# Range checks split and moved, and sums products over two key blocks, in the banded-attention layer of a two-layer kernel

## Chip, cores and metric

The kernel runs on one core of one Trainium2 chip. The time is device microseconds of one execution, and the figure that counts is the median over runs. A core has TensorE (PE in the profile; its weight loads are PEld), VectorE (DVE), ScalarE (ACT), GpSimd (POOL), and SyncE (SP), which issues the DMAs here.

## What is computed

Two layers act on an image of 128 x 256 positions with 256 channels. Each adds an attention over group-normalised input to its input. The first has eight heads, a bias from a second input, a mask and a gate. The change is in the second:

```python
def _L1_conv_ref(x, w_in, b_in, w_out, b_out, band):     # band = 16, H = 4 heads of D = 64
    x2 = x.reshape(B * T, F, C)                          # 128 rows of F = 256 positions, C = 256
    qkv = x2 @ w_in.T + b_in
    q, k, v = jnp.split(qkv, 3, axis=-1)                 # then split into heads
    scores = jnp.einsum('bhid,bhjd->bhij', q, k) / jnp.sqrt(D)
    keep = jnp.abs(i - j) <= band
    scores = jnp.where(keep, scores, -jnp.inf)
    attn = jax.nn.softmax(scores, axis=-1)
    out = jnp.einsum('bhij,bhjd->bhid', attn, v)
    y = out @ w_out.T + b_out

x = x + _L1_conv_ref(_gn(x), ..., 16)
```

Everything is float32.

## The kernel before

The kernel is a fast path with a verdict: it takes exponentials without subtracting a maximum, and checks on the way that the quantities which could leave the safe range did not. Each check leaves a one or a zero per partition in a column of a tile `ok`. At the very end the smallest of them, reduced over the partitions by a product with `ones`, becomes the integer `verdict`; all engines load it and branch to a general kernel if a check failed.

Layer 1 works on pairs of rows, 64 pairs, in a loop over `p` whose order of instructions is written out by hand (`manual_schedule`): each engine runs its instructions in the order of the Python text. In one pass the loop holds three pairs at once. `was` is the pair before, whose second row is still to be applied and put out; `now` is the pair whose scores are taken; `nxt` is the pair whose queries, keys and values are made; `nn` and `n3` are loaded, turned and centred ahead.

The steps that the change touches, or that its effect runs through:

- `scores(r)`: for each row, 256 keys in four blocks of 64. A block's keys meet only `W` = 96 queries, from `q0(k)` on. ScalarE takes the exponential, GpSimd multiplies by the band's ones and zeros (`e<-e,bw`, L1980).
- `apply(r)` (L1998): on tiles of 64 x 32 of the PE array, the products of the values and the exponentials. Even and odd blocks go to different PSUM tiles (`o_eo[0]`, `o_eo[1]`), since neighbours overlap. A third turn of the outermost loop, `a == 2`, multiplies by ones instead of values and gives the softmax sums, into the first half of `su_y`. Every float32 product appears as two matmul records.
- `copy_sums`, `copy_odd` (ScalarE), `join_sums`, `join_odd` (VectorE, L2019 and L2022) add the odd blocks to the even ones; `invert` (L2025) is the reciprocal of the sums; `weigh` (L2030) multiplies the outputs by it.
- `out_block`, `out_row` (L2046) multiply by `w_out` into the second half of `su_y`; `keep_row` (L2054) adds the residual, and the output leaves by DMA.
- `product(n, i)` and `join(n, i)` (L1912 and L1916; L1932): seven products in place of eight for each of queries, keys and values (n = 0, 1, 2). Each n has two PSUM tiles, and a product that starts anew in one waits until its last reader is done.
- `centre`, `differences`, `add_bias`, `turn`: preparing later pairs, on ScalarE (L1865), GpSimd (L1878 to L1881 and L1871) and VectorE (the transpose, L1860).

A check is three VectorE instructions (L958 to L960): a comparison with the lower bound, a `scalar_tensor_tensor` that compares with the upper bound and multiplies, and a minimum. The quantities: the exponentials of the bias (`eb`, 16 checks of 256 columns), the mask (1), the reciprocals of layer 0's sums, loaded again from DRAM (8), and those of layer 1's pairs 0 to 55, also loaded again (4, the last of 128 columns). They wait in the list `checks`, and one is taken out in each pass with `p > 0`, between `nn.centre(0)` and `now.apply(0)`. The last `LATE` = 8 pairs are checked from the tile in place, by `guard`, just ahead of that: 512 columns at once in the loop, and twice 256 columns at the very end.

Of the kernel before, what the change touches and what calls it, by code (L numbers as in the profile page):

```python
# [16 lines left out]
P = 128  # L17
# [756 lines left out]
def fast_kernel(  # L774
# [173 lines left out]
    kb = const.tile([P, KC], F32, name="kb")  # L948
    vb_r = const.tile([P, C], F32, name="vb_r")
    bz_r = const.tile([P, H], F32, name="bz_r")  # L950
    ok = const.tile([P, 48], F32, name="ok")
    done = []

    def check(src, lo, hi, pool):

        n = src.shape[1]
        a = pool.tile([P, 512], F32, name="chk", tag="chk", bufs=1)[:, :n]
        nc.vector.tensor_scalar(a, src, lo, None, ALU.is_gt)  # L958
        nc.vector.scalar_tensor_tensor(a, src, hi, a, ALU.is_lt, ALU.mult)  # L959
        nc.vector.tensor_reduce(ok[:, len(done) : len(done) + 1], a, AX.X, ALU.min)  # L960
        done.append(src)

    def group_pairs(src, g):

# [796 lines left out]
    def q0(k):  # L1761
        return min(max(k * KB - BAND, 0), I - W)

    def half(k):
        return slice((k % 2) * KB, (k % 2 + 1) * KB)
# [15 lines left out]
    with tc.tile_pool(name="l1", bufs=2) as sb, tc.tile_pool(  # L1781
# [54 lines left out]
        class Pair1:  # L1836
# [148 lines left out]
            def apply(self, r):  # L1985


                e = self.es[r]
                for a in range(3):
                    for j in range(NK // 2):  # L1990
                        for h in range(H1):
                            for k in (2 * j, 2 * j + 1):
                                at = slice(h * DH, (h + 1) * DH)
                                n = k % 2
                                to = o_eo[n][at, a, q0(k) : q0(k) + W] if a < 2 else su_eo[n][at, q0(k) : q0(k) + W]
                                w = (self.v[half(k), r, j, h * D1 + a * DH : h * D1 + (a + 1) * DH] if a < 2
                                     else ones[half(k), :DH])
                                nc.tensor.matmul(  # L1998
                                    to, w, e[half(k), h % 2, h // 2, j * W : (j + 1) * W], start=True, stop=True,
                                )  # L2000

            def guard(self, r):
                if self.p == NP - 1:
                    check(self.rv[:, r, :], 1e-16, 1e8, sm)
                elif r == 1 and self.p >= NP - LATE:
                    check(self.rv.rearrange("p r i -> p (r i)"), 1e-16, 1e8, sm)

            def copy_sums(self, r):
                if r == 0:
# [17 lines left out]
            def weigh(self, r):  # L2027
                rv, odd = self.rv, self.odd
                oT = sb.tile([P, 2, I], F32, name="oT1", tag="oT", bufs=3)
                nc.vector.tensor_tensor(oT, odd, bcast(rv[:, r, :], 1, 2), ALU.mult)  # L2030
                self.oT[r] = oT
                if r == 1 and self.p < NP - LATE:
                    nc.sync.dma_start(rsum1[self.p].rearrange("q r i -> q (r i)"), rv[0:P:DH].rearrange("q r i -> q (r i)"))

# [31 lines left out]

        checks = []

        def check_all(src, lo, hi):
            for i in range(0, src.shape[1], 256):
                n = min(256, src.shape[1] - i)
                checks.append(lambda i=i, n=n: check(src[:, i : i + n], lo, hi, sm))

        def load_sums(src, name):
            t = sb.tile([P, src.shape[0] // P], F32, name=name, tag=name, bufs=1)
            nc.sync.dma_start(t, src.rearrange("(a b) -> a b", a=P))
            check_all(t, 1e-16, 1e8)

        with tc.manual_schedule():
            now, nxt = pair1(0), pair1(1)
            now.turn()
            norm1()
            mix_weights()
            for k in range(KC):
                now.centre(k)
            nxt.turn()
            for m in range(KC):
                now.project("qT", m)  # L2090
                now.project("kT", m)
                nxt.centre(m)
            nxt.differences()
            for r in range(2):
                now.values(r)
            now.add_bias()
            nxt.add_bias()
            check_all(eb.rearrange("p h b i -> p (h b i)"), math.exp(-20.0), math.exp(20.0))

            was = Nobody()  # L2100
            for p in range(NP - 1):
                nn = pair1(p + 2) if p == 0 else n3
                n3 = pair1(p + 3)
                if p == 0:
                    nn.turn()
                if p == 1:
                    mask_t = sb.tile([S, I], F32, name="mask_all", bufs=1)
                    nc.sync.dma_start(mask_t, mask)
                    check_all(mask_t, 1e-15, 1e15)
                    load_sums(rsum.rearrange("n q r c i -> (n q r c i)"), "sums0")  # L2110
                if p == NP - LATE + 2:
                    load_sums(rsum1[: NP - LATE].rearrange("n q r i -> (n q r i)"), "sums1")

                now.scores(0)
                now.scores(1)
                was.apply(1)
                nxt.begin_fast()
                was.copy_sums(1)
                nxt.product(0, 1)
                was.copy_odd(1)  # L2120
                nxt.product(1, 1)
                was.join_sums(1)
                for n in range(2):
                    nxt.product(n, 2)
                    nxt.join(n, 2)
                was.invert(1)
                for i in (6, 5, 7):
                    for n in range(2):
                        nxt.product(n, i)
                for n in range(2):  # L2130
                    nxt.join(n, 5)
                was.join_odd(1)
                was.weigh(1)
                was.out_row(0)
                for n in range(2):
                    nxt.product(n, 4)
                    nxt.product(n, 3)
                    nxt.join(n, 3)
                fast = p < NP - 2
                if fast:  # L2140
                    nxt.product(2, 1)
                    nxt.product(2, 2)
                    nxt.join(2, 2)
                nn.centre(0)
                was.guard(1)
                if checks and p > 0:
                    checks.pop(0)()

                now.apply(0)
                now.copy_sums(0)  # L2150
                if fast:
                    nxt.product(2, 6)
                    nxt.product(2, 5)
                now.copy_odd(0)
                now.join_sums(0)
                was.out_block(1, 0)
                if fast:
                    nxt.product(2, 7)
                now.join_odd(0)
                was.out_block(1, 1)  # L2160
                if fast:
                    nxt.join(2, 5)
                was.keep_row(1)
                if fast:
                    nxt.product(2, 4)
                    nxt.product(2, 3)
                    nxt.join(2, 3)
                now.invert(0)
                now.weigh(0)
                nn.centre(1)  # L2170
                nn.differences()
                nn.add_bias()
                n3.turn()
                was, now, nxt = now, nxt, nn
            assert not checks

            now.scores(0)
            was.apply(1)
            was.copy_sums(1)
            was.copy_odd(1)  # L2180
            now.values(0)
            was.join_sums(1)
            was.join_odd(1)
            was.invert(1)
            was.weigh(1)
            was.out_row(0)
            now.scores(1)
            now.values(1, 1)
            was.out_row(1)
            was.guard(1)  # L2190
            now.apply(0)
            now.copy_sums(0)
            now.copy_odd(0)
            now.join_sums(0)
            now.join_odd(0)
            now.invert(0)
            now.weigh(0)
            now.apply(1)
            now.copy_sums(1)
            now.copy_odd(1)  # L2200
            for b in range(NB):
                now.out_block(0, b)
            now.join_sums(1)
            now.invert(1)
            now.join_odd(1)
            now.weigh(1)
            now.keep_row(0)
            now.out_row(1)
            for r in range(2):
                now.guard(r)  # L2210

        tot = sm.tile([P, 1], F32, name="okmin", bufs=1)
        nc.vector.tensor_reduce(tot, ok[:, : len(done)], AX.X, ALU.min)
        ps = mm1("ok_ps")
        nc.tensor.matmul(ps[:, 0:1], ones, tot, start=True, stop=True)
        nc.vector.tensor_scalar(verdict, ps[0:1, 0:1], P - 0.5, None, ALU.is_lt)
# [65 lines left out]
```

## Time and profile before

| what | value |
|---|---|
| median of 3 runs | 3167.43 us (3166.82 to 3171.35) |
| the profiled execution | 3168.69 us, its span 3167.0 us |
| mean granted TensorE clock | 0.982 |
| layer 1's pair loop, from about | 2025 us to 3134 us |
| PE busy | 3027.1 us, 96% of the span |
| DVE busy | 2405.7 us, 76% |
| POOL busy | 2268.8 us, 72% |
| ACT busy | 1572.4 us, 50% |
| DVE instructions | 3983 |
| TensorE matmul records | 35678 |

The profile is of one execution. "Busy" counts the time in which an engine ran an instruction; matmuls are pipelined, so that a busy TensorE is not one at its peak. A line of a timeline gives the start and the length in us, the engine, the line of the kernel, the operation, what it writes and reads, the shapes, and in brackets how long the engine had been idle and what ended that. A line with `x4` merges four instructions. The chain of waits follows the end of the program back to what released each step.

### The profile page before, as it was taken

To read this page: it belongs to the slowest core of one execution; us is meant where nothing else is said; L and a number is where in the kernel's file an instruction comes from. 1 tells how busy PE (TensorE), PEld (TensorE's weight loads), DVE (VectorE), ACT (ScalarE), POOL (GpSimd) and SP (SyncE) were. 2 spreads that over 40 slices of the span, in tenths; PEclk is the share of its full clock that TensorE was granted. 3 is DMA by queue.
4 is the path that set the end of the run, shared out by engine and by line. 5 is a ranking of instruction groups with operands and counts; after the bars stand their busy time and mean duration, and the time that the engine had idled before them with its cause. 6 is when DMAs were issued, how large, how long until landed. Compare 5 with 4: busy or idle time off the path is not lost.

```text
span 3167.0 us, 84680 instructions
## 1 busy us (share of the span) xinstructions
PE 3027.1 (96%) x35678; PEld 2125.0 (67%) x35678; DVE 2405.7 (76%) x3983; ACT 1572.4 (50%) x2637; POOL 2268.8 (72%) x1632
## 2 busy tenths in 40 slices
PE   5579999999999999999999999899999999999997
PEld 3345555556555555556655555688888888888886
DVE  7976677777777777777777777588888777777776
ACT  3454444444444444444444443455555555555553
POOL 3459899889888899988988886455554555554543
PEclk9789999999999999999999999999999999999998
DMA  9952334333333334343243432544343434343431
GB/s 360 392 169 52 98 69 97 98 81 81 95 90 69 98 98 95 71 98 92 66 96 91 98 72 65 123 92 93 91 94 86 99 88 97 89 97 84 102 88 36
DMA packets 690967, 328.42 MB, mean 104 GB/s; under 512 B 538673, under 2 KB 639921, under 8 KB 689425
## 3 DMA queue, kind: packets, MB, share of 16 engines
q1 hardware_dynamic: 686176, 320.28, 40.2%
q8 instruction: 282, 4.62, 0.6%
q10 hardware_dynamic: 4400, 2.63, 0.3%
q14 instruction: 109, 0.88, 0.1%
HBM read 254.09 MB, written 68.75 MB: 102 GB/s over the span
## 4 chain that ended last, share of the span: by engine, by line
PE 87%; DVE 5%; DMA 2%; issue 2%; POOL 2%; ACT 1%; ACTq 0%; DVEq 0%; POOLq 0%; SPq 0%
PE ps_p L1357 21%; PE ps_qk L1916 12%; PE ps_sc L1394 8%; PE ps_ov L1429 7%; PE ps_su_y L2046 7%; PE ps_y L1484 7%; PE ps_v L1375 7%; PE ps_qk L1912 6%; PE ps_su L1437 3%; PE ps_sc L1969 3%; PE ps_o L1998 3%; DMA xa<-in_x_dram 1%; PE ps_su_y L1998 1%; DVE st L1192 1%; DVE chk L959 1%
## 5 line engine op out<-in xcount | busy, mean ns | idle before, releaser
L1418 POOL TENSOR_TENSOR eboth<-e 128x512 f32<-128x512 f32 x512 | 744.7, 1474 | 177.5 <-PE ps_su L1437 96.3
L1414 DVE TENSOR_TENSOR e<-ps_sc,eb 128x1024 f32<-128x1024 f32 x384 | 458.2, 1220 | 289.2 <-ACT ps_sc L1406 289.1
L1406 ACT ACTIVATE ps_sc<-ps_sc 128x1024 f32<-128x1024 f32 x384 | 375.4, 1007 | 436.5 <-PE ps_sc L1394 310.0
L1394 PE MATMUL ps_sc<-qT,kT 32*128 32x256 f32 x4096 | 294.1, 400 | 0.9 <-DVE e L1414 0.9
L1879 POOL TENSOR_TENSOR dT<-xgT,dT 128x256 f32<-128x256 f32 x63 | 45.9, 729 | 332.0 <-ACT xgT L1865 332.0
L2046 PE MATMUL ps_su_y<-w_out,oT 128*128 128x256 f32 x1008 | 257.7, 389 | 13.0 <-DVE sums L2019 11.8
L1980 POOL TENSOR_TENSOR e<-e,bw 128x384 f32<-128x384 f32 x256 | 248.0, 999 | 10.8 <-ACT e L1978 10.8
L1394 PEld LDWEIGHTS ps_sc<-qT,kT 32*128 32x128 f32 x4096 | 185.3, 184 | 103.0 <-issue 90.7
L1484 PEld LDWEIGHTS ps_y<-wo,oT 128*128 128x128 f32 x1024 | 194.3, 190 | 83.9 <-issue 44.5
L1429 PE MATMUL ps_ov<-e,v 128*32 128x256 f32 x4096 | 248.8, 383 | 0.0
L1357 PE MATMUL ps_p<-xnT,wq 128*128 128x512 f32 x512 | 247.6, 606 | 0.8 <-POOL xnT L1344 0.8
L1357 PE MATMUL ps_p<-xgT,wg 128*128 128x512 f32 x512 | 247.3, 605 | 0.1
L1484 PE MATMUL ps_y<-wo,oT 128*128 128x256 f32 x1024 | 242.7, 380 | 3.5 <-POOL oT L1474 2.7
L1375 PE MATMUL ps_v<-wv,xnT 128*128 128x256 f32 x1024 | 242.0, 379 | 1.6 <-ACT xgT L1326 1.6
L1357 PE MATMUL ps_p<-xnT,wk 128*128 128x512 f32 x512 | 240.6, 592 | 0.0
L1375 PEld LDWEIGHTS ps_v<-wv,xnT 128*128 128x128 f32 x1024 | 194.5, 190 | 55.9 <-issue 31.1
L1925 ACT ACTIVATE u<-ps_qk,bin_c 128x256 f32<-128x256 f32 x378 | 174.6, 476 | 98.0 <-PE ps_qk L1916 97.9
L2025 DVE RECIPROCAL rv<-sums 128x256 f32<-128x256 f32 x128 | 223.1, 1743 | 0.0
L2046 PEld LDWEIGHTS ps_su_y<-w_out,oT 128*128 128x128 f32 x1008 | 183.5, 192 | 39.8 <-DVE sums L2019 18.9
L1429 PEld LDWEIGHTS ps_ov<-e,v 128*32 128x32 f32 x4096 | 120.4, 110 | 109.5 <-issue 43.1
L1878 POOL TENSOR_TENSOR dT<-xgT 128x256 f32<-128x256 f32 x63 | 46.5, 738 | 195.4 <-ACT xgT L1865 195.4
L1357 PEld LDWEIGHTS ps_p<-xnT,wk 128*128 128x128 f32 x512 | 97.3, 190 | 122.5 <-issue 122.5
(229 smaller groups left out, 6630.9 us busy)
## 6 DMA issues: line engine op xcount, KB each, us to landing
xa<-in_x_dram SPq DMA_DIRECT2D x8, 4096.0 KB
xt<-in_x_dram SPq DMA_DIRECT2D x64, 512.0 KB
x<-xo SPq DMA_DIRECT2D x16, 2048.0 KB
xt<-x SPq DMA_DIRECT2D x64, 512.0 KB
rvb<-rsum SPq DMA_DIRECT2D x252, 128.0 KB
xs<-x SPq DMA_DIRECT2D x252, 128.0 KB
out_dram<-yo SPq DMA_DIRECT2D x63, 512.0 KB
xs<-in_x_dram SPq DMA_DIRECT2D x248, 128.0 KB
```

The costliest lines, as they stand in the source:

```text
L1357: nc.tensor.matmul(ps, w[:, k, m * P : (m + 1) * P], getattr(self, src)[:, k, :], start=(k == 0), stop=(k == KC - 1),)
L1375: nc.tensor.matmul(self.ps_v[:, b * C : (b + 1) * C], self.xnT[:, k, t * P : (t + 1) * P], wv[:, k, :], start=(k == 0), stop=(k == KC - 1),)
L1394: nc.tensor.matmul(self.pss[q // 2][:, q % 2, b, :], self.kT[rs, c, r * I + b * P : r * I + (b + 1) * P], self.qT[rs, c, r * I : (r + 1) * I],
L1406: nc.scalar.activation(self.pss[a], ps, AF.Exp)
L1414: nc.vector.tensor_tensor(es[a], pss[a], eb[:, h : h + 2], ALU.mult)
L1418: nc.gpsimd.tensor_tensor(t, es[a][:, :, 0, :], es[a][:, :, 1, :], ALU.add)
L1429: nc.tensor.matmul(ov[q * D0 : (q + 1) * D0, c, :], self.v[:, r, b, h * D0 : (h + 1) * D0], es[q // 2][:, q % 2, b, :], start=(b == 0), st ...
L1484: nc.tensor.matmul(self.ps_y[:, b * C : (b + 1) * C], self.oT[r][:, k, b * P : (b + 1) * P], wo[:, k, :], start=(k == 0), stop=(k == KC - 1),)
L1916: nc.tensor.matmul(to, lhs, rhs, start=start, stop=True, skip_group_check=True)
L1980: nc.gpsimd.tensor_tensor(e[:, q], e[:, q], bcast(bw.rearrange("p b w -> p (b w)"), 1, KC), ALU.mult)
L2025: nc.vector.reciprocal(self.rv[:, r, :], self.sums)
L2046: nc.tensor.matmul(self.y[:, b], self.oT[r][:, k, b * P : (b + 1) * P], w_out[:, k, :], start=(k == 0), stop=(k == KC - 1),)
```

## The change

A check now consists of two entries of a list. `low` is the comparison with the lower bound and the minimum of its result; the other is a plain maximum of the source, kept in a second row of `ok`. The comparison of the maxima with the upper bound is made later for many columns at once (`below`): for the columns of `eb` and the mask at the end of pass p = 32, and for all others at the end. Entries for the reciprocals of the last eight pairs go into a second list, `late`, at the end of `weigh`, 256 columns for each row; `some_checks(n)` takes `n` entries, those of `late` first.

The entries are taken in other places of the pass: one behind `was.invert(1)` and one behind `now.join_odd(0)` in every pass with p > 0; from p = 57 also two in the old place and one at the end of the pass. Behind the loop two are taken ahead of the last `apply(1)`, and all that are left at the end.

In `apply` the sums leave the common loop. For each head and each parity of blocks one product takes both key blocks: the moving operand has 2 x 96 columns, and the output two stretches of 96 columns, `gap` = 112 apart.

```diff
-    ok = const.tile([P, 48], F32, name="ok")
...
-        nc.vector.tensor_scalar(a, src, lo, None, ALU.is_gt)
-        nc.vector.scalar_tensor_tensor(a, src, hi, a, ALU.is_lt, ALU.mult)
-        nc.vector.tensor_reduce(ok[:, len(done) : len(done) + 1], a, AX.X, ALU.min)
...
+    ok = const.tile([P, 2, 48], F32, name="ok")
...
-                for a in range(3):
+                gap = q0(2) - q0(0)
+                for a in range(2):
...
+                for h in range(H1):
+                    for n in range(2):
+                        two = su_y[h * DH : (h + 1) * DH, n].rearrange("p a i -> p (a i)")
+                        nc.tensor.matmul(
+                            two[:, q0(n) : q0(n) + 2 * gap].rearrange("p (j w) -> p j w", w=gap)[:, :, :W],
+                            ones[half(n), :DH],
+                            e[half(n), h % 2, h // 2, :].rearrange("p (j w) -> p j w", w=W), start=True, stop=True,
+                        )
...
-            def guard(self, r):
-                if self.p == NP - 1:
-                    check(self.rv[:, r, :], 1e-16, 1e8, sm)
-                elif r == 1 and self.p >= NP - LATE:
-                    check(self.rv.rearrange("p r i -> p (r i)"), 1e-16, 1e8, sm)
...
                 self.oT[r] = oT
+                if self.p >= NP - LATE:
+                    look(late, self.rv[:, r, :], 1e-16)
...
+        checks, late, cols = [], [], [0]
+        nc.gpsimd.memset(ok, 1.0)
+
+        def look(queue, src, lo):
+
+            at = cols[0]
+            cols[0] += 1
+
+            def low():
+                above = sm.tile([P, I], F32, name="above", tag="above", bufs=1)[:, : src.shape[1]]
+                nc.vector.tensor_scalar(above, src, lo, None, ALU.is_gt)
+                nc.vector.tensor_reduce(ok[:, 0, at : at + 1], above, AX.X, ALU.min)
+
+            queue += [low, lambda: nc.vector.tensor_reduce(ok[:, 1, at : at + 1], src, AX.X, ALU.max)]
+
+        def look_all(src, lo):
+            for i in range(0, src.shape[1], I):
+                look(checks, src[:, i : min(i + I, src.shape[1])], lo)
+
+        def below(start, stop, hi):
+            nc.vector.tensor_scalar(ok[:, 1, start:stop], ok[:, 1, start:stop], hi, None, ALU.is_lt)
+
+        def some_checks(n):
+            for _ in range(n):
+                queue = late or checks
+                if queue:
+                    queue.pop(0)()
...
                 was.invert(1)
+                some_checks(p > 0)
                 for i in (6, 5, 7):
...
                 nn.centre(0)
-                was.guard(1)
-                if checks and p > 0:
-                    checks.pop(0)()
+                some_checks(2 if p > NP - LATE else 0)
 
                 now.apply(0)
...
                 now.join_odd(0)
+                some_checks(p > 0)
                 was.out_block(1, 1)
...
                 n3.turn()
+                some_checks(p > NP - LATE)
+                if p == NP // 2:
+                    below(0, n_eb, math.exp(20.0))
+                    below(n_eb, n_mask, 1e15)
                 was, now, nxt = now, nxt, nn
...
             was.out_row(1)
-            was.guard(1)
             now.apply(0)
...
             now.weigh(0)
+            some_checks(2)
             now.apply(1)
...
             now.out_row(1)
-            for r in range(2):
-                now.guard(r)
+            some_checks(len(checks) + len(late))
+            below(n_mask, cols[0], 1e8)
 
         tot = sm.tile([P, 1], F32, name="okmin", bufs=1)
-        nc.vector.tensor_reduce(tot, ok[:, : len(done)], AX.X, ALU.min)
+        nc.vector.tensor_reduce(tot, ok.rearrange("p a n -> p (a n)"), AX.X, ALU.min)
```

## The prediction

> **What bounds the kernel now.** I read the page's busy shares first, then a table of windows over single passes of layer 1's pair loop, then timelines of VectorE and GpSimd inside one pass, and last the chain of waits.
>
> ```profile
> PE 3027.1 (96%) x35678; PEld 2125.0 (67%) x35678; DVE 2405.7 (76%) x3983; ACT 1572.4 (50%) x2637; POOL 2268.8 (72%) x1632
> ```
>
> TensorE is the bound, so an edit on VectorE is worth only what it makes TensorE wait. Windows over a pass with an old check, a pass without one, and a late pass with two:
>
> ```profile
> 2239.50:2257.10 17.60, 17.51 (x330) 15.38 (x328) 14.66 (x23) 9.84 (x23) 9.49 (x9) 1.00 0.39 92
> 2488.00:2505.40 17.40, 17.40 (x330) 15.44 (x328) 13.33 (x21) 9.88 (x23) 9.50 (x9) 1.00 0.41 95
> ...
> 3055.30:3076.90 21.60, 19.61 (x331) 17.19 (x331) 16.16 (x26) 9.87 (x22) 9.43 (x9) 0.90 0.35 75
> ```
>
> Columns: window, length, then busy us of PE, PEld, DVE, ACT, POOL, then the granted clock. By the output's DMA issues, which come once a pass, one without a check takes 17.37 us, one with a check 17.61. So an old check costs 0.24, in the 25 passes p = 1 to 25. The passes p = 57 to 61 end 0.9, 3.2, 4.2, 4.1 and 1.8 us over 17.37: 14.2 together. The reason stands in the timeline of the first window:
>
> ```profile
> 2252.24 0.87 DVE L959 SCALAR_TENSOR_TENSOR chk<-eb,chk 128x256 f32<-128x256 f32 x1
> ...
> 2253.14 0.42 DVE L960 TENSOR_REDUCE ok<-chk 128x1 f32<-128x256 f32 x1
> ...
> 2253.48 0.41 DVE L2019 TENSOR_TENSOR sums<-ps_su_y,sums 128x256 f32<-128x256 f32 x1
> ...
> 2253.95 0.73 PEld L2046 LDWEIGHTS ps_su_y<-w_out,oT 128*128 128x128 f32 x4 [0.28 <-DVE sums L2019]
> ```
>
> The check stands in front of `join_sums`, and TensorE's `out_block` waits for that. From p = 57 on the check is 512 wide and mostly followed by a second; TensorE idles 1.96 to 1.99 us there three times, and each time the next 3.4 us are granted at 0.50. A fourth idle time of 1.63 us leaves the clock at 1.00.
>
> **What the new places look like.** VectorE's and GpSimd's timelines of a pass without a check:
>
> ```profile
> 2510.73 1.74 DVE L2025 RECIPROCAL rv<-sums 128x256 f32<-128x256 f32 x1
> 2512.98 0.42 DVE L1932 TENSOR_TENSOR qT<-ps_qk,u 128x256 f32<-128x256 f32 x1 [0.51 <-ACT u L1925]
> ...
> 2514.47 1.20 DVE L2030 TENSOR_TENSOR oT<-odd,rv 128x512 f32<-128x512 f32 x1
> ...
> 2516.20 0.41 DVE L1932 TENSOR_TENSOR qT<-ps_qk,u 128x256 f32<-128x256 f32 x1
> ```
>
> ```profile
> 2508.95 2.36 POOL L1871 TENSOR_TENSOR xt<-xt,bout_r 128x1024 f32<-128x1024 f32 x1
> 2511.26 3.86 POOL L1980 TENSOR_TENSOR e<-e,bw 128x384 f32<-128x384 f32 x4
> ```
>
> Place A, behind `was.invert(1)`, has 0.51 us free (2512.47 to 2512.98). From 2512.98 on VectorE has no gap until the last line of the first block, the join of product 3, ends at 2516.61. TensorE's weight load for product (2,2) starts at 2516.66, just behind it: what A adds beyond 0.51 lengthens the pass. Place B, behind `join_odd(0)`, has 0.67 us free and GpSimd is idle there. Place E, the end of the pass, has nothing free: the transpose ends at 2509.56 and `join_sums(1)` starts at 2509.48, under GpSimd's bias add.
>
> **The change, part by part.** A check is split into a low half (comparison 0.28, minimum 0.42: 0.75 with gaps) and a high half (one maximum, 0.45). The `scalar_tensor_tensor`, 0.43 alone and 0.83 to 1.00 beside GpSimd, goes. Popping the queues by hand: 25 low halves fall on A and 25 high ones on B in p = 1 to 25; from p = 57 two halves stay in the old place, one each at A and B, and a low half at E.
>
> *Lock.* Does the comparison wait for GpSimd? The comparison's own row (L958) never shows it: 282 to 295 ns at 256 columns, but it always began before GpSimd did. The nearest row that shows it is layer 0's:
>
> ```profile
> L1295 DVE TENSOR_SCALAR lrs<-lmv x64: 169/1069/1114, 196.8 to 1916.8; 128x4 f32<-128x4 f32 x64
> ```
>
> 169 ns alone, 1069 in the middle; in the one at 904.50 it ends at 905.57, just past the end of the first of two GpSimd operations back to back (each 1.25). The Trainium skill, "SBUF — State Buffer", section on the two separate sides, gives the rule: VectorE in a two-port mode and GpSimd exclude each other for a whole instruction, and its list of who takes the pair says that `tensor_reduce` never does. That the mode is on here the trace supports: from 256 to 512 columns the comparison grows by 0.133 us (0.283 to 0.416), the minimum by 0.266 (0.420 to 0.686). By L958's row alone A costs 0.75 - 0.51 = 0.24 and E about 0.5; by the rule both comparisons stand behind GpSimd. I take the rule.
>
> *A, low half, 25 passes.* The comparison is ready at 2512.49, waits for GpSimd's second multiply (about 2513.2), ends 2513.36; the minimum ends 2513.8; the joins, `join_odd` (0.35, 0.35 and 0.71 apart) bring `weigh` to 2515.2. There it no longer waits for GpSimd (2515.12), and takes 0.69 instead of 1.20. So the last join is about 0.25 late, not 0.75. Net of the old check: 25 x (0.25 - 0.24) = 0. Lower bound 0 a pass, upper bound under the rivals. Behind the wait stand the joins, and TensorE's product (2,2) waits for them. *B*: 0.45 inside 0.67, nothing; without that cover it would delay a join whose reader, product (2,3), has 0.2 us of room.
>
> *Late passes.* A high half at A fits (0.45), a low half at p = 57 costs 0.25. The old place now holds 1.2 us against 1.56 in the checked pass above, which was 0.28 late: nothing, or 0.1. E at p = 57 to 60: the comparison waits for the bias add until 2511.31, ends 2511.46, the minimum 2511.9, `join_sums(1)` 2512.26, the join of product 2 at 2512.6; product (0,5) wanted its weights at 2510.8. TensorE idles 1.8 us. Lower bound 0.3 (no lock), upper 3.5 (half clock for 3.4 us behind it). The Trainium skill, "TensorE: Matmul & The Clock Gate", part 1, has the clock fall after an idle window of about 3.4 us; here 1.96 us was enough and 1.63 was not. By the page no loss, by the trace 1.8 lies between: I take none, and keep 4 x 1.7 for the range. Sum: 0.3 + 0.1 + 4 x 1.8 = 7.6 against 14.2: -6.6. At p = 62 a shorter old place (-0.5) and E (+0.5) cancel.
>
> *`below`, once at p = 32*: two tiny comparisons at E, behind the bias add and then a multiply: +2.0 (0.3 to 4).
>
> *Sums products.* Per row 32 records of 96 columns become 16 of 192, columns the same. The chain of waits, layer 1's sums and layer 0's:
>
> ```profile
> 2500.93 0.37 PE ps_su_y L1998 x22
> ```
>
> ```profile
> 911.05 0.86 PE ps_su L1437 x16
> ```
>
> With the few that mix with `ps_o`, the sums take about 0.39 a row, 12.2 ns a record. Layer 0's 256-column records on four tiles take 53.8 ns, 0.84 ns a column and tile; on eight tiles 192 columns are 20.2 ns, 16 of them 0.32. Saved: 0.065 a row, 128 rows: -8.3. Bounds 0 (a row limited otherwise) and 0.1. The same page's floor, about 25 ns from start to start of small matmuls (part 1), would make it 16 x 25 ns = 0.4 a row and 51 in all; 12.2 ns a record contradicts it, so I leave it out. ScalarE's copy and the rest stand behind the last sum as before.
>
> *Instructions.* 64 of some 660 TensorE instructions a pass go. Its waits put down to "issue" before these sums are 8.2 us in the loop; a tenth is -0.8 (0 to -2).
>
> *Tail.* Dropping the check at 3144 lets `join_odd(0)` start after ScalarE's copy, 0.43 earlier; two halves (1.2) then stand before `join_sums(1)`: output weights 0.85 later. At the end stood six instructions, 3156.56 to 3159.03, 2.47. Now eight halves are left: four maxima and two low halves at 256, one check at 128 (0.9), a `below` (0.2), minimum over 96 instead of 38: about 4.5. The verdict ends the span 6.9 us later as before; the last output packet lands at 3158.4, earlier than the verdict at 3160.1, so nothing hides it. Together 0.85 + 2.05 = +2.9. SP's and POOL's queues get nothing but one memset at the layer's start.
>
> **Sum.** 0 - 6.6 + 2.0 - 8.3 - 0.8 + 2.9 = -10.8. The profiled execution took 3168.69 (span 3167.0), 1.26 above the median 3167.43: 3157.9 on its scale, about 3157 for a median.
>
> **Rivals.**
> *Free places.* If the comparison doesn't wait for GpSimd, E costs some 0.5 a pass, `below` 0.3: the late part gives -12, the sum is -18, 3149. For it: L958 has never waited. Against it: L1295.
> *Sums gain nothing.* If the row is limited by dispatch and skew, not columns, 8.3 goes: 3165, no measurable change. For it: the records' uneven starts.
> *Slower: A holds.* If at A the comparison is not let in between GpSimd's four multiplies but waits for all (2515.12), the joins come some 2.1 late in each of 25 passes: +46 on mine, 3203. It decides from about 0.9 us a pass. Against it: L1295 got in between two GpSimd operations back to back.
>
> **Chances.** Anything within 0.2% (6.3 us) is about what a measurement of this kernel can't tell from no change. Mine 0.45 (3150 to 3165 alone; faster 0.36, same 0.09); free places 0.22 (faster); sums nothing 0.20 (faster 0.03, same 0.16, slower 0.01); A holds 0.13 (slower 0.12, same 0.01). Faster 0.61, same 0.26, slower 0.13. The range 3144 to 3170 leaves out "A holds" and the far end of "free places".
>
> **What would show it.** Right: passes 1 to 25 still near 17.6 less 0.1, with the comparison at A near 0.9 us and `oT` near 0.7; passes 26 to 56 near 17.24; comparisons of about 2 us at E and TensorE idle 1.8 before product (0,5) in p = 58 to 61; about 2 us more between the last `yo` and the verdict. Wrong: comparisons of 0.28 everywhere (free places), 17.37 in passes 26 to 56 (sums), comparisons near 2.8 at A (slower).

## The result and the profile after

The changed kernel takes 3147.8 us (median of 4 runs, 3147.36 to 3149.58), the kernel before 3167.12 us in the same sitting (4 runs, 3164.29 to 3171.35): a ratio of 0.9939, 95% interval 0.9922 to 0.9956. That is faster, by 19.3 us where 10.8 were forecast. The profiled executions stand 21.3 us apart in their spans (3167.0 and 3145.6 us); every table and list of waits below is of such single executions, while "measured" times are medians.

The page's busy row and the windows over single passes, with columns as before. The first window is a pass with a low half at place A, the second a pass without a check, the third a late pass with a low half at place E:

```profile
PE 3020.1 (96%) x33630; PEld 2099.2 (67%) x33630; DVE 2406.7 (77%) x4007; ACT 1573.3 (50%) x2637; POOL 2270.8 (72%) x1633
```

```profile
2239.50:2257.00 17.50, 17.43 (x298) 15.07 (x297) 14.31 (x24) 9.87 (x23) 9.55 (x10) 1.00 0.41 90
2488.00:2505.40 17.40, 17.40 (x298) 15.09 (x297) 13.40 (x21) 9.87 (x22) 9.51 (x9) 1.00 0.41 93
...
3043.30:3062.20 18.90, 17.43 (x296) 14.91 (x296) 16.46 (x28) 9.87 (x22) 9.49 (x10) 1.00 0.39 85
```

TensorE is still busy 96% and VectorE has lost nothing. In the late pass the clock is granted at 1.00, where before it was 0.90.

To see where the 21.3 us went, I took the intervals between the output's DMA issues on SyncE's queue, one to a pass (L2062 before, L2054 after), and split each stretch into its usual length, the median, and what single passes lie above it ("irregular"). The first interval belongs to p = 2.

| stretch | before | after | difference |
|---|---|---|---|
| up to the first output DMA | 2042.4 | 2039.4 | -3.0 |
| p = 2 to 25, usual pass | 24 x 17.62 | 24 x 17.50 | -2.9 |
| p = 26 to 56, usual pass | 31 x 17.38 | 31 x 17.38 | -0.1 |
| p = 2 to 56, irregular | 12.3 | 2.0 | -10.3 |
| p = 57 to 62 | 117.5 | 109.2 | -8.4 |
| from there to the end | 33.0 | 36.3 | +3.3 |

The differences add up to the 21.3 us but for rounding.

Half of the gain is in none of the usual passes. It is in some passes of the kernel before that took 0.2 to 1.5 us more than their neighbours, and that are nearly gone after. Their cause stands in the list of waits over the pair loop (2042 to 3110 us; total, times, longest), at "issue": TensorE stood still there, and no other engine, DMA or semaphore in that list accounts for it. Before, then after:

```profile
PEld ps_su_y L1998 <- issue: 9.7, 14, 1.5
PE ps_su_y L1998 <- issue: 6.5, 10, 1.3
```

```profile
PEld ps_su_y L1992 <- issue: 1.9, 6, 0.6
...
PE ps_su_y L1992 <- issue: 0.2, 1, 0.2
```

The rows of weight loads and products overlap and are not to be added. Both are at the sums products.

**The checks.** Lines of VectorE's timeline, place A:

```profile
2239.05 1.02 DVE L2071 TENSOR_SCALAR above<-eb 128x256 f32<-128x256 f32 x1
2240.11 0.42 DVE L2072 TENSOR_REDUCE ok<-above 128x1 f32<-128x256 f32 x1
...
2241.83 0.69 DVE L2020 TENSOR_TENSOR oT<-odd,rv 128x512 f32<-128x512 f32 x1
```

and GpSimd's at the same time:

```profile
2235.65 2.36 POOL L1861 TENSOR_TENSOR xt<-xt,bout_r 128x1024 f32<-128x1024 f32 x1
2237.98 3.92 POOL L1970 TENSOR_TENSOR e<-e,bw 128x384 f32<-128x384 f32 x4
```

The comparison takes 1.02 us instead of 0.28 and ends at 2240.07, just past the second of four multiplies (2237.98 + 2 x 0.98 = 2239.94). It is let in between two of them, and `oT` no longer has to wait. Place E, VectorE and GpSimd:

```profile
3039.55 1.24 DVE L1850 STREAM_TRANSPOSE xT<-xs 128x1024 f32<-128x1024 f32 x1
3040.71 1.98 DVE L2071 TENSOR_SCALAR above<-rv 128x256 f32<-128x256 f32 x1
```

```profile
3040.18 2.35 POOL L1861 TENSOR_TENSOR xt<-xt,bout_r 128x1024 f32<-128x1024 f32 x1
```

The comparison ends at 3042.69, 0.16 behind the bias add. TensorE's timeline shows what that costs:

```profile
3043.86 1.99 PE L1906 MATMUL ps_qk<-dT,wst 128*128 128x256 f32 x8 [1.52 <-DVE qT L1922]
```

The minimum behind the comparison at A runs beside GpSimd's third multiply and takes 0.42 us, as everywhere. The maxima on `eb`, 407 to 410 ns, say nothing of a lock here: GpSimd is idle at place B.

### The profile page after: what moved, and what is told of

Same layout as the page of the kernel before. It is cut to its first block, busy times and chain, and to the rows that moved or that the text cites. A ratio compares the mean times of both kernels' runs of the same rounds, so it can differ in the third digit from the quotient of the medians.

```text
span 3145.6 us, 80608 instructions
## 1 busy us (share of the span) xinstructions
PE 3020.1 (96%) x33630; PEld 2099.2 (67%) x33630; DVE 2406.7 (77%) x4007; ACT 1573.3 (50%) x2637; POOL 2270.8 (72%) x1633
## 4 chain that ended last, share of the span: by engine, by line
PE 84%; DVE 8%; DMA 2%; issue 2%; POOL 2%; ACT 1%; ACTq 0%; DVEq 0%; POOLq 0%; SPq 0%
PE ps_p L1347 21%; PE ps_sc L1384 8%; PE ps_qk L1906 8%; PE ps_ov L1419 7%; PE ps_y L1474 7%; PE ps_v L1365 7%; PE ps_qk L1902 7%; PE ps_su_y L2038 6%; PE ps_o L1984 3%; PE ps_su L1427 3%; PE ps_sc L1959 3%; PE ps_su_y L1992 2%; DVE rv L2015 2%; DMA xa<-in_x_dram 1%; DVE st L1182 1%
## 5 line engine op out<-in xcount | busy, mean ns | idle before, releaser
L1906 PE MATMUL ps_qk<-dT,wst 128*128 128x256 f32 x756 | 174.8, 380 | 7.1 <-DVE qT L1922 7.1
```

The source lines that it names most:

```text
L1906: nc.tensor.matmul(to, lhs, rhs, start=start, stop=True, skip_group_check=True)
```

## The experiments

Three things needed testing: which part brought the 10.3 us of irregular time and why; why the sums' saving shows in no usual pass; and whether the lock of VectorE and GpSimd is what places A and E cost. "Irregular" below is that of p = 2 to 56.

### The parts alone

`e1_sums` is the kernel before with only the new sums products (the diff's part of `apply`):

```diff
-                for a in range(3):
+                for a in range(2):
...
+                for h in range(H1):
+                    for n in range(2):
...
+                        two = su_y[h * DH : (h + 1) * DH, n].rearrange("p a i -> p (a i)")
...
```

> The kernel before with the wide sums products alone; the old three-instruction checks stay in their old places. Theory (instruction supply): the wide sums take 64 of some 660 TensorE instructions out of a pass and with them the irregular waits for instructions, so that the excess of single passes over the usual length falls from 12.3 us in passes 2 to 56 to about 2, while the usual length stays at 17.61 with a check and 17.37 without; passes 57 to 61 stay near 14 us over. About 10 to 12 us faster than before. Rival (the checks' new places did it): the irregular waits stay near 12 us and this run is within 2 us of before. My prediction's own account (fewer starts of matmuls) wants 17.24 in passes 26 to 56.

Measured: 3156.27 us, ratio 0.9965 (0.9953 to 0.9978).

`e2_checks` is the changed kernel with the old sums products, so the checks alone:

```diff
-                for a in range(2):
+                for a in range(3):
...
-                for h in range(H1):
-                    for n in range(2):
...
```

> The changed kernel with the old sums products: split and moved checks alone. Theory: passes 1 to 25 at 17.50 (from 17.61), passes 58 to 61 near 18.95, the end 3.3 us longer, as in the changed kernel, but the irregular waits for instructions back at about 12 us: 8 to 11 us faster than before, so that this and the sums alone add up to the change. Rival (the checks' places remove the irregular waits): near the changed kernel, 19 us faster than before.

Measured: 3159.92 us, ratio 0.9976 (0.9967 to 0.9985); 6.5 us faster where 8 to 11 were expected.

| kernel | usual pass, p = 2 to 25 | p = 26 to 56 | irregular | p = 57 to 62 |
|---|---|---|---|---|
| before | 17.62 | 17.38 | 12.3 | 117.5 |
| `e1_sums` | 17.61 | 17.37 | 3.0 | 114.1 |
| `e2_checks` | 17.52 | 17.39 | 12.8 | 109.2 |
| after | 17.50 | 17.38 | 2.0 | 109.2 |

Each part is a gain, some 10 and 6.5 us against 19 together; what is missing to 19 lies within the intervals. The irregular time belongs to the sums, the 0.1 us of early passes and most of the late ones to the checks. The sums leave the usual pass alone.

The 3.4 us that `e1_sums` gains in the late passes are the clock's. Three idle times of TensorE of 1.97, 1.97 and 1.98 us stand there as before, but only the last was followed by half clock, and two of the passes take 19.5 us instead of 20.6 and 21.6. So the length of an idle time alone does not decide.

### Which sums: burst or count

If TensorE runs short of instructions because there are too many in all, wide products in either row of a pair should bring half. If it runs short only where many short ones follow each other, it matters in which row they are. Ahead of the second row's sums stand 64 records of scores and 64 of values (`scores(1)` and `apply(1)`), with no long product between; ahead of the first row's, the 64 of values alone, and before them long products. `e5_wide_row0` takes two key blocks at once in the first row alone, as below; `e6_wide_row1` has `r == 1` in its place. Both have the same number of instructions.

```diff
+                if r == 0:
+                    for h in range(H1):
+                        for n in range(2):
...
+                else:
+                    for j in range(NK // 2):
+                        for h in range(H1):
+                            for k in (2 * j, 2 * j + 1):
...
```

> The changed kernel, with the wide sums products in the first row's apply alone; the second row's, which stands right behind 64 score records, keeps the narrow ones. A pass has 32 TensorE instructions fewer than before (a weight load and a matmul for each of 16 records), half of what the change takes out. Burst theory (TensorE runs out of instructions where short ones follow each other longest, scores and apply of the second row): irregular excess over the usual pass in passes 2 to 56 stays near that of the narrow kernel, 10 us or more. Count theory (what matters is the number of instructions in a pass): between the two, 5 to 8 us.

> The mirror of the run before: wide products in the second row's apply alone, the same number of instructions. Burst theory: irregular excess near that of the changed kernel, 2 to 3 us, and the time within 3 us of it. Count theory: the same 5 to 8 us as the run before.

Measured: `e5_wide_row0` 3156.22 us, ratio 0.9968 (0.9955 to 0.998); `e6_wide_row1` 3150.78 us, 0.9955 (0.9938 to 0.9971). Irregular 10.5 and 2.7 us. The waits of both, over the same stretch as above:

```profile
PEld ps_su_y L2002 <- issue: 10.4, 13, 1.5
PE ps_su_y L2002 <- issue: 7.7, 11, 1.3
```

```profile
PEld ps_su_y L1993 <- issue: 3.0, 7, 0.9
...
PE ps_su_y L1993 <- issue: 1.0, 3, 0.5
```

In the first L2002 are the narrow products, left in the second row, and they stall as before; in the second L1993 are the wide ones. Against the 12.8 us of `e2_checks`, the same 1024 records less bring 2.3 us in one row and 10.1 in the other. So it is the row, not the count. The intervals of the two ratios overlap, but each of the 4 runs of `e6_wide_row1` (at most 3152.56 us) is faster than each of the 6 of `e5_wide_row0` (at least 3153.37). The profiled execution of `e6_wide_row1` was its fastest, 3147.29 us, 3.5 below its median, so its profile flatters it. Yet all eleven profiles agree: narrow sums in the second row go with 10.5 to 14.4 us of irregular time (4 kernels), wide ones with 2.0 to 4.5 (6 kernels; `e8_best` has 7.0, with a wait of its own shown below). That the second row matters for the length of its burst is the likeliest reading; the rows differ in their neighbours too.

What starves TensorE in the burst is argued rather than shown, but the traces point to the fetching of its instructions. Each of the 14 waits of the weight loads before begins 1.0 to 2.4 us after the start of a 16 KB packet of the instruction queue q8 and ends 2.3 to 3.0 us after it, though these packets are 6.8 us apart (median). The page counts 282 packets before and 266 after: 16 less for 4096 weight loads and matmuls less, so 256 instructions to a packet (an estimate). By it, 7 passes of the kernel before, with 659 weight loads and matmuls each, fill 18.0 packets, and 3 passes of `e1_sums`, with 595, fill 7.0. The long passes recur at just these distances: p = 2, 9, 16, 23, 30, 37, 44, 51, and again 4, 11, 18 and so on before; p = 4, 7, 10 and 41, 44, 47, 50 in `e1_sums`. And every pass with such a wait in `e6_wide_row1` (p = 5, 14, 23, 25, 34, 43, 54) has one in `e5_wide_row0` too. No run changed the fetching alone.

### The lock

`e3_high_first` puts the maximum first in each check, so that at A, in the passes up to 56, and at E it is the maximum that runs beside GpSimd, and the comparison falls to other places:

```diff
-            queue += [low, lambda: nc.vector.tensor_reduce(ok[:, 1, at : at + 1], src, AX.X, ALU.max)]
+            queue += [lambda: nc.vector.tensor_reduce(ok[:, 1, at : at + 1], src, AX.X, ALU.max), low]
```

> The changed kernel with the two entries of a check in the other order: the maximum first, then the comparison with its minimum. The maximum then falls on the place behind invert(1) in passes 1 to 25 and on the end of the pass in the late ones, the low half behind join_odd(0). Theory (a comparison waits while GpSimd holds the port pair, a maximum does not): passes 1 to 25 fall from 17.50 to 17.37 (-3), passes 58 to 61 from 18.95 to 17.5 or less (-5 to -6), the end is 0.6 longer; comparisons take 0.28 us behind join_odd(0): 7 to 9 us faster than the changed kernel. Rival (what counts is VectorE time at these places, whatever the instruction): a maximum of 0.4 at the end of the pass still costs about 0.3 a pass, and the first 25 passes stay near 17.5.

Measured: 3139.45 us, ratio 0.9915 (0.9898 to 0.9931). VectorE's timeline at place A:

```profile
2238.11 0.36 DVE L2074 TENSOR_REDUCE ok<-eb 128x1 f32<-128x256 f32 x1
...
2240.19 1.04 DVE L2020 TENSOR_TENSOR oT<-odd,rv 128x512 f32<-128x512 f32 x1
```

GpSimd's multiplies ran meanwhile, and all sixteen maxima on `eb` are alike (min/median/max in ns):

```profile
2236.82 3.86 POOL L1970 TENSOR_TENSOR e<-e,bw 128x384 f32<-128x384 f32 x4
```

```profile
L2074 DVE TENSOR_REDUCE ok<-eb x16: 359/360/363, 2029.0 to 2290.0; 128x1 f32<-128x256 f32 x16
```

At E the maximum takes 0.38 us under the bias add. The comparisons on `eb`, at B now, take 282 to 285 ns, all sixteen. The usual early pass is 17.38, like one without a check, and passes 58 to 61 take 17.5 instead of 18.95. Both costs were the comparison's wait. `oT` is the one that waits at A again, as in the kernel before.

### Why the sums' saving was not seen

TensorE's timeline around the first row's sums, before and after. The `x30` and `x14` lines are the bulk of the sums, the last line is the product behind them:

```profile
2500.62 0.24 PE L1998 MATMUL ps_su_y<-e,ones 64*32 64x96 f32 x1
...
2500.70 0.60 PE L1998 MATMUL ps_su_y<-e,ones 64*32 64x96 f32 x30
2501.23 1.16 PE L1912 MATMUL ps_qk<-wst,dT 128*128 128x128 f32 x8
```

```profile
2506.96 0.32 PE L1992 MATMUL ps_su_y<-e,ones 64*32 64x192 f32 x1
...
2507.04 0.59 PE L1992 MATMUL ps_su_y<-e,ones 64*32 64x192 f32 x14
2507.56 1.16 PE L1902 MATMUL ps_qk<-wst,dT 128*128 128x128 f32 x8
```

The starts of the records behave as forecast: (0.60 - 0.24) / 29 = 12.4 ns apart before, (0.59 - 0.32) / 13 = 20.8 ns after, and first to last start they take 0.44 and 0.35 us. But a wide record is 0.08 longer, and the next product starts 0.25 us behind the last start instead of 0.17. From the first sum to the next product it is 0.61 against 0.60 us; in the second row, by the same reading, 0.64 against 0.60. Some 0.05 us of a pass are saved, not 0.13. The starts are measured; the ends of records are modelled by the profiler, so that the next product stands behind the longer record is a reading and was not tested by itself.

Even these don't shorten the usual pass. TensorE's timeline of product (2,2), the last ahead of `apply(0)`, before and after:

```profile
2516.16 1.21 PE L1912 MATMUL ps_qk<-w_in,xgT 128*128 128x128 f32 x8
2517.30 0.93 PE L1998 MATMUL ps_o<-e,v 64*32 64x96 f32 x60
```

```profile
2505.08 1.27 PE L1902 MATMUL ps_qk<-w_in,xgT 128*128 128x128 f32 x8
2506.28 0.93 PE L1984 MATMUL ps_o<-e,v 64*32 64x96 f32 x60
```

What TensorE saves earlier in the pass it waits here: counted from the pass's first record of `apply(0)`, this product's first weight load comes at 16.01 us before and at 15.97 after, and the pass ends at 17.38 in both. It starts anew in a tile that VectorE's join must have read. The join stands behind `join_odd`, `oT` and `yo`, and `oT` waits for GpSimd's multiplies (1.20 us instead of 0.69), which stand behind the bias add of 2.36. To test that, `e4_bias` moves the bias add between two of GpSimd's differences, where GpSimd waited for ScalarE anyway:

```diff
-            def differences(self):
+            def differences(self, bias=False):
...
+                if bias:
+                    self.add_bias()
...
-                nn.differences()
-                nn.add_bias()
+                nn.differences(True)
```

> The changed kernel with GpSimd's bias add (2.36 us) issued between the first and the second of the four differences instead of behind them, where GpSimd waits 5 us for ScalarE anyway. Theory (the usual pass of 17.37 is set by a ring: ScalarE's centring, GpSimd's differences, bias add and multiplies, VectorE's weigh that waits for the last multiply, yo, the join of product 3, TensorE's product (2,2), and round again; TensorE's own saving is lost there): with the ring 2.36 us shorter weigh takes 0.69 instead of 1.26, the join comes earlier, product (2,2) does not wait, and a pass of the middle falls below 17.37 by 0.15 to 0.25, 10 to 15 us in all. Rival (TensorE's own work sets the pass): the middle passes stay at 17.37.

Measured: 3128.37 us, ratio 0.9877 (0.9861 to 0.9894), 19 us below the changed kernel where 10 to 15 were expected. GpSimd's and TensorE's timelines:

```profile
2485.42 0.73 POOL L1868 TENSOR_TENSOR dT<-xgT 128x256 f32<-128x256 f32 x1 [5.11 <-ACT xgT L1855]
2486.10 2.37 POOL L1861 TENSOR_TENSOR xt<-xt,bout_r 128x1024 f32<-128x1024 f32 x1
2491.02 0.73 POOL L1871 TENSOR_TENSOR dT<-xgT,dT 128x256 f32<-128x256 f32 x1 [2.56 <-ACT xgT L1855]
```

```profile
2483.61 1.05 PE L1904 MATMUL ps_qk<-w_in,xgT 128*128 128x128 f32 x8
```

Product (2,2) is down from 1.27 to 1.05, and the usual pass from 17.38 to 17.17: the whole difference of the pass, 0.21, is at this one product. `oT` takes 0.69 us in every one. Passes with a check at A are 17.17 too, from 17.50, and passes 58 to 61 are 17.60, from 18.95, since the comparison at E no longer meets the bias add and takes 0.62 us instead of 1.98: these two bring the rest.

If that is right, the sums' saving must show once the wait is gone. `e7_bias_narrow` is `e4_bias` with the old sums products:

```diff
-                for h in range(H1):
-                    for n in range(2):
...
+                for j in range(NK // 2):
+                    for h in range(H1):
+                        for k in (2 * j, 2 * j + 1):
...
```

> The kernel with GpSimd's bias add moved, but with the old narrow sums. In the changed kernel the wide sums left the usual pass at 17.38, since the ring over GpSimd set it. Theory: with the ring out of the way TensorE sets the pass, and the 0.047 us that both rows' wide products save (0.008 and 0.039 by the traces) shows: the usual pass is 17.20 to 17.24 instead of 17.167; the irregular waits come back at about 10 us besides: 12 to 14 us slower than with wide sums. Rival: the usual pass stays at 17.167, TensorE's saving is lost in yet another wait.

Measured: 3143.66 us, ratio 0.9931 (0.9915 to 0.9948), 15.3 above `e4_bias` where 12 to 14 were expected; the profiled executions stand 13.6 apart. The usual pass is 17.23, 0.06 over that of `e4_bias`, and the irregular time 14.4 against 4.5 us. Over 55 passes this is 3.3 and 9.9, nearly all of the 13.6.

### A version that beats both

`e8_best` has the order of `e3_high_first` and the bias add of `e4_bias`. It loads layer 1's first sums already at p = 40, so that fewer checks are left at the end, and takes those that are left while VectorE waits for the last row's output, ahead of `out_row(1)`:

```diff
+                if p == 40:
+                    load_sums(rsum1[:32].rearrange("n q r i -> (n q r i)"), "sums1a")
...
-            some_checks(2)
             now.apply(1)
...
             now.keep_row(0)
+            some_checks(len(checks) + len(late))
             now.out_row(1)
-            some_checks(len(checks) + len(late))
```

> All that the runs point to, put together: wide sums, the maximum of a check ahead of its low half, GpSimd's bias add between the differences, the sums of layer 1 loaded again in two parts (pairs 0 to 31 at p = 40, 32 to 55 at p = 58), and the entries left over after the loop taken while VectorE waits for the last output row instead of behind it. Theory: middle passes 17.17, passes 57 to 61 below 17.4, and the end 3 to 4 us shorter since VectorE had 3.3 us idle there: 3120 to 3124. Rival: the leftover entries delay the last yo by as much as they leave the end: no better than 3126.

Measured: 3126.8 us, ratio 0.9878 (0.9862 to 0.9895); more than expected. The tail had come down, but one pass took 21.06 us. VectorE's timeline there:

```profile
2705.03 0.42 DVE L2076 TENSOR_REDUCE ok<-sums1a 128x1 f32<-128x256 f32 x1 [3.71 <-DMA sums1a<-rsum]
```

By p = 40 the queue of checks was empty, so place A of the same pass took the first check of a load that had only just been issued. `e9_best2` puts the checks into the queue one pass after the load:

```diff
                 if p == 40:
-                    load_sums(rsum1[:32].rearrange("n q r i -> (n q r i)"), "sums1a")
+                    sums1a = load_sums(rsum1[:32].rearrange("n q r i -> (n q r i)"), "sums1a")
+                if p == 41:
+                    look_all(sums1a, 1e-16)
```

> The kernel of e8_best with one edit: the first load of layer 1's sums is still issued at the start of pass 40, but its two range checks enter the queue one pass later, so that VectorE cannot meet them before the load has landed. Theory (VectorE waited on a DMA that had just been issued): the idle 3.71 us ahead of the maximum of sums1a is gone, the interval of pair 38 falls from 21.06 to about 17.2 us, and the time from 3126.8 to about 3123 us; a ratio to before of about 0.9863. Rival (the long pass is an instruction fetch of TensorE that falls there by chance, and the load only lies beside it): an interval of about 21 us stays at that pair, or turns up nearby, and the time stays within 1 us of 3126.8.

Measured: 3123.86 us (4 runs, 3123.49 to 3125.09), ratio 0.987 (0.9854 to 0.9887). The pass is 17.17 us, the idle time is gone, and the time is 2.9 us lower. The end of the layer on VectorE, after and in `e9_best2`:

```profile
3133.68 0.69 DVE L2046 TENSOR_TENSOR yo<-ps_y,xt 128x512 f32<-128x512 f32 x1 [3.27 <-PE ps_y L2038]
3134.29 0.41 DVE L2074 TENSOR_REDUCE ok<-rv 128x1 f32<-128x256 f32 x1
...
3137.88 0.25 DVE L2231 TENSOR_REDUCE okmin<-ok 128x1 f32<-128x96 f32 x1
```

```profile
3113.38 0.42 DVE L2074 TENSOR_REDUCE ok<-above 128x1 f32<-128x256 f32 x1
3113.72 0.68 DVE L2048 TENSOR_TENSOR yo<-ps_y,xt 128x512 f32<-128x512 f32 x1
...
3114.52 0.25 DVE L2235 TENSOR_REDUCE okmin<-ok 128x1 f32<-128x96 f32 x1
```

From the start of the last `yo` to the final minimum it is 4.2 us in the first and 0.8 in the second: the checks fill the 3.27 us in which VectorE waited for that output.

## Why the prediction was right or wrong

The forecast of 3157 us had the sign right and the amount too small; 3147.8 lies in its range. That is in part luck. Its sum of -10.8 came from the wrong places: half of the gain stands in a term put at 0.8. And 3147.8 is below all of its own account's 3150 to 3165, next to the 3149 of the rival "free places", whose mechanism the runs refute. By its own steps, against the table of intervals:

- **A, forecast 0; measured -2.9.** The mechanism is as described: a comparison of about 1 us let in between two multiplies, `oT` down to 0.69. Only the size was off: the pass grows by 0.12 and not by 0.25.
- **B, forecast 0; confirmed.** The maximum takes 0.41 us there, and `e3_high_first` shows that a comparison has room too.
- **Late passes, forecast -6.6; measured -8.4.** At E TensorE stands still 1.52 us instead of 1.8, so a pass pays 1.58. Another 0.6 is p = 62, 15.83 us instead of 16.44, where a gain and a loss were said to cancel. The clock stays at 1.00, as taken; but the ground given, that 1.96 us is enough to halve it, is too simple: `e1_sums` has two idle times of 1.97 us that left it at 1.00.
- **`below`, forecast +2.0; measured +1.1.** Behind the bias add it took 1.87 us, but only 1.06 of it reached the end of the pass (18.44 against 17.38).
- **Sums, forecast -8.3; measured about 0 in the usual pass.** This is the step that failed, and the rival "sums gain nothing" had its outcome in the usual pass, though not its reason: the starts of the records do follow the columns. Two errors lie in it. The term counted columns and left out that the next product stands behind the longer last record, 0.08 us a row: 0.05 a pass, not 0.13. And it took TensorE's saving to be the pass's. The prediction had itself read that product (2,2) starts just behind a join of VectorE; it used this to charge place A, and not to ask what the same wait makes of a faster TensorE. `e4_bias` and `e7_bias_narrow` show that this wait is what the saving turned into. The floor of about 25 ns from start to start (the Trainium skill, "TensorE: Matmul & The Clock Gate", part 1) was rightly left out: 12.4 and 20.8 ns both lie under it.
- **Instructions, forecast -0.8 (0 to -2); measured about -11.** The mechanism was named and its size missed by more than ten. With the 1.1 of `below` taken out, the irregular time went from 12.3 to about 1 us. A tenth of the waits was taken since a tenth of the instructions goes, that is, by count; `e5_wide_row0` and `e6_wide_row1` show that it goes by where they stand. The rows by "issue" also summed to less than the passes lost: the intervals between the output DMAs would have shown the 12.3 us.
- **Tail, forecast +2.9; measured +3.3.**
- **Not forecast: -3.0 ahead of the first output DMA.** Over all eleven kernels this moment lies between 2039.0 and 2042.4 us, in no order that follows the edits of layer 1. Its cause is open.

The other rivals fell. "Free places" is refuted by the 1.02 and 1.98 us comparisons, "A holds" by the comparison that was let in after the second of four multiplies.

The Trainium skill, "SBUF — State Buffer", section on the two separate sides, had decided the lock for the forecast, and the runs agree with it in both directions: the two-port comparison waits (1.02 and 1.98 us against 0.28) and the reduction does not (0.36 to 0.38 us for the maximum at A and E in `e3_high_first`, and 0.42 for the minimum, beside GpSimd as without it).

## What to carry to other kernels

A saving on the busiest engine counts only up to the next thing that engine waits for inside the same loop pass, so look for that wait and size it before multiplying a saving by the number of passes. Look at the spread of the passes as well as at the usual one: here 12 us lay in a few long passes, which mostly went when a long run of short matmuls was made shorter at its end. And where an engine shares a lock with another, put the instruction that never takes the lock beside the other engine, and the one that does where the other engine is idle.

## What the runs showed of the hardware that was not expected

- TensorE stood still in the second row's stretch of short matmuls, for up to 1.5 us at a time, and passes ran 12.3 us over their usual length in 55 passes. Making 32 records into 16 at the end of that stretch took nearly all of it away, and doing the same in the first row little (12.8 to 10.5). The waits end 2.3 to 3.0 us after the start of a 16 KB instruction packet and recur every 7 passes before and every 3 in `e1_sums`, as whole numbers of packets do; that they are waits for instructions was not tested by itself.
- With matmul records of 192 columns in place of two of 96, 0.08 us longer, the next full-array product came 0.25 us behind the last start instead of 0.17.
- VectorE's comparison was let in between two GpSimd instructions that stand back to back, and ended 0.15 us behind the one it had waited for, at A and at E.
- Idle times of about 2 us halved TensorE's clock or did not. Stretches of half clock in the pair loop last 3.41 us and start whole multiples of 3.41 us apart (3052.68, 3073.16 and 3093.64 us before). On that raster, the idle times that were followed by half clock (three before, one in `e1_sums`) put 1.96 to 1.99 us into one step, the two of 1.97 in `e1_sums` that were not put at most 1.55. That is read from these traces; no run moved an idle time on purpose.
